# Graph sums one group ahead, exponential factors from the messages product, paced vector work: a graph layer in fp32 on one core

## The chip, the cores and the metric

One core of one Trainium2 chip. The metric is the time of the device in microseconds, the median of the runs. All runs named below are of state fast (undisturbed), and the runs of one kernel agree within 0.4%. The experiments were run in three sittings on three chips, in which the median of the kernel before was 2544.1 (experiments 1 to 4), 2541.0 (5 to 8) and 2543.3 us (9 to 12): a difference of a few us between two of them is noise.

Engine names as in the profile: PE is TensorE's matmuls, PEld its weight loads, DVE VectorE, ACT ScalarE, POOL GpSimd, SP SyncE, which issues the DMAs. PSUM is the memory that TensorE writes its results to; a buffer there is free again when another engine has read it (evacuated it). In the code P = 128 is the number of partitions, NT = 4 the row blocks of a batch, ND = 2 its channel blocks, B = 32, G = 4 batches in a group, NG = 8 groups.

## The reference, cut to what matters

Batches b of 32, each 512 rows of 256 channels. All in fp32.

```python
h = maximum(layernorm(x), 0)
# convolution branch
c = relu(bn1(conv1(h)));  c = bn2(conv2_17_taps(c));  x_conv = relu(h + c)
# graph branch
s    = h @ w_se.T + b_se                        # 3 columns
sq   = sum(s * s, -1)
A    = exp(-(sq[:, None] + sq[None, :] - 2 s @ s.T)) * adj      # 512 x 512
msg  = relu(h @ w_msg.T + b_msg)
x_nmp = A @ msg
# gates: a GRU cell on concat(x_conv, x_nmp) and h, then out = x + cell
```

## The kernel before: the parts that the change touches

Four batches make a group. conv2 of a group is 25 products, each written as two halves (`yield "pe", 1.65`). The rest of the work, here the graph and the gates of the batches of the group before, is a Python generator, and a balance counter `ahead` decides which of the two is emitted next. Each engine is handed its instructions in the order of emission.

The graph stage of one batch, in the order of emission. `positions` of this batch has been emitted in the middle of the gates of the batch before.

```python
def positions(b):                                   # 2 matmuls of 512 columns, four small evacuations
    matmul_sum(ps[:67, :], [(wse[:, i, :], HB[b][:, i, :]) for i in range(ND)])
    ... left[0:3], right[0:3], right[32:35], left[64:67] ...
...
for c in range(NT):                                 # NT = 4
    if c % 2 == 0:
        messages(b, msg, c)
        yield 1.8
    kernel_exp(at, c)                               # one 67-row product of 512 columns, Exp on ScalarE
    yield 0.87
    masked(b, at, c)                                # 4 transposes of the mask, one multiplication on VectorE
    yield 0.55
    if waiting and c % 2:
        finish(*waiting[0], c - 1)                  # output transposes of the batch before
        yield 0.55
```

All four mask row blocks of a batch are one tile of 1 MB, loaded a batch ahead. x has three buffers: three loads are asked for together and their norms follow one after another, so most loads are well ahead of their norm (VectorE waits for an x 6 times, 18.2 us in all). Norm pieces are handed out by `norm_some()`, pieces of the sums of conv2 by `sum_some()`, without a common budget. PSUM: three buffers for conv2, three for the other products, two for transposes.

## Time and profile before

2544.1 us median (2538.2 to 2545.3). What matters for the argument:

| | before |
|---|---|
| TensorE busy | 2386.9 us of 2542.4 |
| TensorE idle | 155 us: 71 in the first 260 us, 63 up to 2250 us, the rest in the tail |
| mean granted clock | 0.973 |
| TensorE work at full clock, by start-to-start times | some 2323 us |
| VectorE busy | 1224.5 us (48%) |

How to read it: span = work at full clock + idle TensorE + the rest of the busy time, most of which the lower clock adds. The lines that carry this stand in the prediction.

### The profile page before, as it was taken

How to read it: one execution, taken by the hardware profiler on the slowest of the kernel's cores; microseconds unless marked ns; L12 is line 12 of the kernel's file. 1: busy time of each engine (PE TensorE's matmuls, PEld its weight loads, DVE VectorE, ACT ScalarE, POOL GpSimd, SP SyncE). 2: the span in 40 equal slices, each digit the busy share in tenths (PEclk: the TensorE clock that was granted, in tenths of full speed). 3: DMA queues.
4: the chain of work that ended last, by engine and by line, in shares of the span. 5: the costliest groups of instructions: out<-in, count | busy, mean ns of one | idle time of the engine just before them, and what ended most of it. 6: DMA issues, size and time to landing. Idle time of an engine off the chain costs nothing.

```text
span 2542.4 us, 20857 instructions
## 1 busy us (share of the span) xinstructions
PE 2386.9 (94%) x8192; PEld 1484.4 (58%) x8192; DVE 1224.5 (48%) x1766; ACT 646.4 (25%) x882; POOL 335.2 (13%) x240
## 2 busy tenths in 40 slices
PE   6678999999999999999999999999999999999998
PEld 4564566655665656655666566665666655665444
DVE  7984543454445444454444554445543454543222
ACT  2332223132132222222212322223212132222222
POOL 1000111111111111112110121100211011111111
PEclk9888999999999999999999999999999999999999
DMA  5233222322232222322223321332222222221110
GB/s 213 114 148 113 85 83 91 116 83 75 83 109 90 91 83 83 124 70 83 87 90 117 99 87 65 106 100 91 91 83 91 91 83 75 91 92 49 42 42 25
DMA packets 108996, 231.15 MB, mean 91 GB/s; under 512 B 8418, under 2 KB 57698, under 8 KB 108258
## 3 DMA queue, kind: packets, MB, share of 16 engines
q1 hardware_dynamic: 108898, 229.82, 26.5%
q8 instruction: 64, 1.05, 0.2%
q14 instruction: 34, 0.28, 0.0%
HBM read 183.13 MB, written 46.66 MB: 90 GB/s over the span
## 4 chain that ended last, share of the span: by engine, by line
PE 83%; DVE 13%; ACT 1%; issue 1%; DMA 1%; POOL 0%; SPq 0%; POOLq 0%; DVEq 0%
PE ps_acc L86 55%; PE ps_c L86 20%; PE ps_acc L488 3%; PE ps_tr L86 2%; DVE x L239 2%; DVE x L242 2%; DVE y L346 2%; PE ps_tr L508 2%; PE ps_tr L496 1%; PE ps_tr L217 1%; DVE at L497 1%; DVE msg L483 1%; DVE z L346 1%; DVE z L353 0%; DVE st L182 0%
## 5 line engine op out<-in xcount | busy, mean ns | idle before, releaser
L86 PEld LDWEIGHTS ps_c<-x,w 128*128 128x128 f32 x3200 | 612.6, 193 | 172.3 <-issue 142.7
L86 PE MATMUL ps_c<-x,w 128*128 128x228 f32 x3200 | 685.1, 360 | 23.7 <-DVE z L368 10.5
L86 PE MATMUL ps_acc<-hTb,whh 128*128 128x512 f32 x768 | 360.2, 594 | 2.0 <-DVE xnmp L502 2.0
L86 PE MATMUL ps_acc<-xconv,wih 128*128 128x512 f32 x768 | 361.3, 593 | 0.0
L86 PE MATMUL ps_acc<-xnmp,wih 128*128 128x512 f32 x768 | 360.6, 592 | 0.0
L599 POOL TENSOR_TENSOR gate_t<-hTb,r 128x512 f32<-128x512 f32 x64 | 88.0, 1375 | 1857.9 <-issue 1260.3
L86 PEld LDWEIGHTS ps_acc<-xnmp,wih 128*128 128x128 f32 x768 | 145.3, 189 | 184.3 <-issue 184.3
L580 DVE SCALAR_TENSOR_TENSOR r<-ps_acc,vec,r 128x512 f32<-128x512 f32 x64 | 48.0, 751 | 413.5 <-ACT r L578 413.5
L86 PEld LDWEIGHTS ps_acc<-xconv,wih 128*128 128x128 f32 x768 | 146.2, 190 | 158.1 <-issue 157.7
L86 PE MATMUL ps_acc<-at,msg 128*128 128x512 f32 x512 | 230.7, 594 | 2.1 <-DVE at L497 2.0
L592 DVE TENSOR_TENSOR r<-ps_acc,r 128x512 f32<-128x512 f32 x64 | 44.3, 692 | 389.8 <-PE ps_acc L86 389.8
L86 PEld LDWEIGHTS ps_acc<-hTb,whh 128*128 128x128 f32 x768 | 143.4, 190 | 124.8 <-issue 119.8
L242 DVE SCALAR_TENSOR_TENSOR x<-x,x 128x471 f32<-128x471 f32 (+1 forms) x184 | 165.1, 897 | 5.1
L86 PEld LDWEIGHTS ps_acc<-at,msg 128*128 128x128 f32 x512 | 97.0, 190 | 109.4 <-issue 103.1
L239 DVE TENSOR_TENSOR x<-x 128x471 f32<-128x471 f32 x200 | 157.5, 804 | 1.4
L86 PE MATMUL ps_acc<-wmsg,hTb 128*128 128x256 f32 x512 | 137.5, 417 | 0.0
L488 PE MATMUL ps_acc<-right,left 67*128 67x512 f32 x256 | 133.9, 604 | 0.0
L588 ACT ACTIVATE z<-ps_acc,brz 128x512 f32<-128x512 f32 x64 | 44.0, 687 | 342.5 <-PE ps_acc L86 342.5
L497 DVE TENSOR_TENSOR at<-ps_tr,at 128x512 f32<-128x512 f32 x128 | 86.5, 687 | 87.5 <-ACT at L489 83.9
L578 ACT ACT_TABLE_LOAD x32 | 41.1, 1283 | 339.2 <-PE ps_acc L86 339.2
L593 ACT ACTIVATE r<-r,vec 128x512 f32<-128x512 f32 x64 | 46.2, 722 | 300.7 <-DVE r L592 300.7
L502 DVE COPY xnmp<-ps_acc 128x512 f32<-128x512 f32 x64 | 44.2, 691 | 158.7 <-PE ps_acc L86 158.6
(90 smaller groups left out, 2213.1 us busy)
## 6 DMA issues: line engine op xcount, KB each, us to landing
w<-wd SPq DMA_DIRECT2D x175, 512.0 KB, 3.4
m_sb<-in_adj_dram SPq DMA_DIRECT2D x32, 1024.0 KB, 6.1
x_sb<-in_x_dram SPq DMA_DIRECT2D x32, 512.0 KB, 6.1
hd<-hT SPq DMA_DIRECT2D x32, 512.0 KB, 3.0
hTb<-hd SPq DMA_DIRECT2D x32, 512.0 KB, 6.7
y<-in_x_dram SPq DMA_DIRECT2D x64, 256.0 KB, 4.0
out_dram<-y SPq DMA_DIRECT2D x64, 256.0 KB, 2.2
wd<-w SPq DMA_DIRECT2D x25, 512.0 KB, 2.6
```

The source lines that it names most:

```text
L86: nc.tensor.matmul(ps, lhsT, rhs, start=(i == 0), stop=(i == len(pairs) - 1))
L239: nc.vector.tensor_tensor(dst, get(a), get(b), op=ALU.subtract)
L242: nc.vector.scalar_tensor_tensor(dst, a, -2.0, b, op0=ALU.mult, op1=ALU.add)
L346: SUMS.append(lambda: nc.vector.tensor_tensor(dst, a, b, op=op))
L488: nc.tensor.matmul(ps, left[:, c * P : (c + 1) * P], right, start=True, stop=True)
L497: nc.vector.tensor_tensor(at[:, c, :], ps, at[:, c, :], op=ALU.mult)
L502: nc.vector.tensor_copy(xnmp[:, d, :], ps)
L508: nc.tensor.transpose(ps[:, j, d * P : (d + 1) * P], o_sb[:, d, (c + j) * P : (c + j + 1) * P], ident)
L580: nc.vector.scalar_tensor_tensor(r, ps_h, vec[:, _COL["b_hh"] + 2 * ND + o : _COL["b_hh"] + 2 * ND + o + 1], r, op0=ALU.add, op1=ALU.mult,)
L592: nc.vector.tensor_tensor(r, ps_n, r, op=ALU.add)
L593: nc.scalar.activation(r, r, AF.Tanh, bias=vec[:, _COL["b_ih"] + 2 * ND + o : _COL["b_ih"] + 2 * ND + o + 1],)
L599: nc.gpsimd.tensor_tensor(t, hT[:, o, :], r, op=ALU.subtract)
```

## The change

Intent: take work off TensorE, the bound, and even out VectorE's work. The positions product disappears into three more columns of the messages product. The four exponent products of a batch, 5 rows deep, run in four row groups of the array at once. For that the graph of a batch is made together with its rows, a group before its gates, and its sums wait in DRAM. A pacer hands out VectorE's work by credit. To fit, x goes from three buffers to two, the mask from one 1 MB tile to three of 256 KB, conv2 from three PSUM buffers to two.

The diff, cut to its core (cuts marked):

```diff
-    cps = ... bufs=3 ...            # conv2's PSUM
-    acc = ... bufs=3 ...
+    cps = ... bufs=2 ...
+    acc = ... bufs=4 ...
-        XS[b] = front.tile([P, NT, D], F32, name="x_sb", bufs=3)
+        XS[b] = front.tile([P, NT, D], F32, name="x_sb", bufs=2)
+    def load_masks(upto):
+        for k in range(len(MS), min(upto, B * NT)):
+            MS[k] = front.tile([P, N], F32, name="m_sb", bufs=3)
+            nc.sync.dma_start(MS[k], adj[k // NT, k % NT * P : (k % NT + 1) * P, :])
 ... (positions and its constants removed; w_se and b_se become columns 256 to 258 of wmsg and bmsg)
+    def kernel_exp(at):
+        pss = [acc.tile([P, N], F32, name="ps_acc") for c in range(NT)]
+        for c in range(NT):
+            k = slice(32 * c, 32 * c + 5)
+            nc.tensor.matmul(
+                pss[c], left[k, :], right[k, :], start=True, stop=True, tile_position=(32 * c, 0)
+            )
+        for c in range(NT):
+            nc.scalar.activation(at[:, c, :], pss[c], AF.Exp)
+    def masked(b, at, n):
+        ... four transposes of MS[b * NT + n], one multiplication ...
+        load_masks(b * NT + n + 4)
+    def begin(b):
+        for d in range(ND):
+            norm_t(b, d)                            # transposes of the normalized x
+            yield 0.55
+        if b + 2 < B:
+            load(b + 2)
+            NORMS[b + 2] = norm(b + 2)              # from here on the pacer may issue it
+    def graph(b, between=()):
+        ... gap(): the next piece of `between`, or a sign that asks for half a conv2 product ...
+        for c in range(NT):
+            messages(b, msg, c)                     # also writes the 3 columns of s
+            yield 0.93
+        factors()                                   # 5 short VectorE instructions
+        yield gap()                                 # filler: in steady state half a conv2 product
+        yield gap()
+        factors_t()                                 # 5 transposes, two copies on ScalarE
+        yield 0.67
+        yield gap()
+        kernel_exp(at)
+        yield 1.2
+        yield from finish_waiting()
+        yield gap()
+        for n in range(NT):
+            masked(b, at, n)
+            yield 0.55
+        yield gap()
+        ... graph sums, copied by ScalarE, stored to DRAM ...
+    def pace(pe):
+        credit = min(credit + pe * 0.8, 4.0)
+        kinds = (sum_next, operand_some, norm_next, prepare_next)
+        while credit > 0:
+            ... issue the next piece of the next kind that has one ...
+            credit -= 0.9
 ... (gates read the sums from DRAM; conv2's weights of all 25 products are made before its first product)
```

## The prediction

> **What bounds the kernel now.** I read the page first: busy shares, then the slices.
>
> ```profile
> PE 2386.9 (94%) x8192; PEld 1484.4 (58%) x8192; DVE 1224.5 (48%) x1766; ACT 646.4 (25%) x882; POOL 335.2 (13%) x240
> ...
> PE   6678999999999999999999999999999999999998
> ...
> DVE  7984543454445444454444554445543454543222
> ...
> PEclk9888999999999999999999999999999999999999
> ```
>
> TensorE is the bound from the fifth slice on. In the first three (190 us) it is 60 to 80% busy and VectorE is the busy one. Next the groups of instructions, TensorE only; the count is of instructions, and one fp32 matmul is two of them.
>
> ```profile
> L86 PE MATMUL ps_c<-x,w 128*128 128x228 f32 x3200 | 685.1, 360 | 23.7 <-DVE z L368 10.5 <-DVE z L370 6.7 <-DVE x L239 3.9
> ...
> L488 PE MATMUL ps_acc<-right,left 67*128 67x512 f32 x256 | 133.9, 604 | 0.0
> ...
> L496 PE MATMUL ps_tr<-ident,m_sb 128*128 128x128 f32 x512 | 77.0, 272 | 0.8 <-DVE at L497 0.8
> L86 PE MATMUL ps_tr<-hTb,wse 128*67 128x512 f32 x128 | 61.9, 607 | 15.5 <-DMA hTb<-hd 15.5
> L508 PE MATMUL ps_tr<-ident,o_sb 128*128 128x128 f32 x256 | 44.7, 303 | 76.2 <-DVE at L497 70.1 <-POOL o_sb L601 5.5
> ```
>
> The means include about 0.17 us of pipeline that overlaps the next matmul, so I take costs from start to start in the timeline. Columns there: start, us, engine, line, operation.
>
> ```profile
> 1001.33 1.70 PE L86 MATMUL ps_c<-x,w 128*128 128x228 f32 x8
> 1002.87 1.88 PE L86 MATMUL ps_tr<-hTb,wse 128*67 128x512 f32 x4
> 1004.58 1.88 PE L86 MATMUL ps_acc<-hTb,whh 128*128 128x512 f32 x4
> ...
> 1053.90 1.02 PE L488 MATMUL ps_acc<-right,left 67*128 67x512 f32 x2
> 1054.76 0.60 PE L496 MATMUL ps_tr<-ident,m_sb 128*128 128x128 f32 x4
> 1055.20 1.02 PE L488 MATMUL ps_acc<-right,left 67*128 67x512 f32 x2
> ```
>
> So four instructions of 512 columns take 1.71 us (0.43 each), eight of 228 take 1.54, one exponent product 0.86, four transposes 0.44. Per batch at full clock: conv2 100 x 0.1925 = 19.25; gates 72 x 0.43 = 30.9; graph sums 16 x 0.43 = 6.9; messages 3.46; conv1 3.44; exponents 4 x 0.86 = 3.44; positions 1.72; mask transposes 1.76; the other transposes 1.76. Sum 72.6 us, by 32 batches 2323 us. The span of 2542 is then 2323 of work, 155 of idle TensorE (2542.4 - 2386.9) and some 64 of busy time at a lower clock.
>
> Where the loss sits: the windows of the first 260 us show 71 us idle and about 15 us lost to the clock, 86 in all. From 260 to 2250 us TensorE waits 63 us, of which 61 are this line:
>
> ```profile
> PE ps_tr L508 <- DVE at L497: 61.1, 18, 6.2
> ```
>
> and a stall costs more than itself. Five-microsecond windows round one of 3.00 us (after the times: TensorE busy, loads, VectorE, ScalarE, GpSimd, clock, DMA share, GB/s):
>
> ```profile
> 885.00:890.00 5.00, 5.00 (x25) 4.21 (x24) 3.44 (x4) 2.23 (x3) 3.78 (x3) 1.00 0.30 105
> 890.00:895.00 5.00, 2.00 (x12) 1.27 (x11) 4.93 (x5) 2.03 (x4) 1.79 (x1) 0.84 0.00 0
> 895.00:900.00 5.00, 5.00 (x15) 4.20 (x15) 3.51 (x12) 0.00 (x0) 0.00 (x0) 0.50 0.16 52
> ```
>
> The clock fell to half for the next 5 us: 2.5 us more lost.
>
> **What the Trainium skill says.** "TensorE: Matmul & The Clock Gate", Part 3, says row tiles at 32-row steps run concurrently, and gives 3.07x for four of K=32, N=512. It also says matmuls start and end strictly in program order. No row tiling is in this trace, so nothing here confirms either. The same page, Part 1, says the clock halves after about 3.4 us without matmul work, and Part 4 that transposes do not count as such work. The windows above agree: a 3.00 us stall between transposes sufficed. "TensorEngine Tiling (Array Packing)", Key Properties, says a change of tiling mode drains TensorE; not shown here, and I allow two pipeline depths of the 0.17 us seen above, 0.35 us a batch.
>
> **The change part by part.**
>
> 1. Positions product removed: 32 x 1.72 = -55 us. Its result now comes from three more columns of the messages product: 259 for 256 columns, +1 us.
>
> 2. Exponents: 32 x 3.44 = 110 us removed. In their place four products of 5 rows in four row groups. An fp32 product is two instructions on the same rows. If all groups overlap fully, a batch costs two passes, 0.86 + 0.35 = 1.2 us. If starts stay in program order (both passes of group 0, then both of group 1), the second pass of one group overlaps only the first of the next: five passes, 5 x 0.43 + 0.2 = 2.35 us. I take 1.7, +54 us.
>
> 3. Five new transposes a batch for the factors: 5 x 0.11 = 0.55, +18 us.
>
> TensorE work: 2323 - 55 + 1 - 110 + 54 + 18 = 2231 us.
>
> 4. Startup. The weights of all 25 conv2 products and the graphs of four batches are now done before the first conv2 product. VectorE in the first stage (to the end of group 0): weight taps 52 us (the sum of their rows); norms of 10 batches by 4.0; graphs of 8 batches by some 6.4 (messages, factors, four masks of 0.69); one group's operands (53 us, an eighth of their rows); most of one group's sums (30 us). About 226 us, and it cannot start on weights before their 4.4 MB have landed, near 20 us. TensorE's work in that stage is 16 graph-row units of the first and second group, about 150, and conv2's 77: also some 227. Neither can be fully busy. I expect 60 idle and 15 of clock loss, 75 against 86.
>
> 5. The middle. The 61 us of boundary waits go, since operand, norm and sum pieces are now issued at 0.8 of TensorE's pace, where before a row of 2.1 us pieces stood ahead of the mask multiplication. But the exponents no longer lie between the mask transposes. Of a batch's four masks, three have buffers ahead; the load of the fourth (256 KB) is issued only after the transposes of the first. The same size lands in 2.1 at least and 3.7 us in the median for the residual loads. Transpose 1 at 0, transpose 2 at 0.44, the third waits for a PSUM buffer until the first multiplication ends (0.6 + 0.69 + wake-up, about 1.45), the fourth for its mask, 0.6 + 2.7 = 3.3. It ends near 3.75 for 1.76 of work: 2.0 lost, and with a piece or two of VectorE work between, 2.2. Four conv2 halves are taken as filler before it, so the balance counter is negative there and no conv2 lies between the masks. Besides: 0.5 waiting for the factors (five short VectorE instructions behind paced ones), 0.3 for the exponentials (a table load of 1.28 and four of 0.6, against 0.88 + 1.54 + 0.88 of cover), and some 1.0 of clock, as 3.75 us with only transposes is the case of the windows above less often. Sum 4.0 a batch by 28 batches outside the startup's first group: 112 us. Other waits of conv2, which has two PSUM buffers instead of three, and of the first load of gates (one of 15.5 us before): 15.
>
> 6. The tail. The last four batches are gates alone. The output transposes now come after one product of 1.72 us of the next batch; they need the last gate: 0.69 + 0.72 + three GpSimd instructions of some 1.5 = 5.9 us. So 4.5 idle three times, with 1 of clock each, about 7 where the last sums and evacuations are waited for, and the 5.5 of the end as before: 29, with clock 33.
>
> 7. Graph sums through DRAM: 64 stores and loads of 256 KB, some 33 MB more on queues that were 26.5% busy: hidden. The copy of 0.69 moves from VectorE to ScalarE, which is 25% busy: no cost.
>
> Sum: 2231 + 75 + 112 + 15 + 33 = 2466 us, a ratio of 0.969 to the 2544 of before.
>
> **The rivals.**
>
> A, the author's arithmetic: row groups fully concurrent (-16 us from my figure) and paced work leaving almost no wait, graphs 1 us a batch (-84), startup 15 better: 2350. For it: VectorE is only 48% busy, and the pace spreads its work. Against: the fourth mask's load, which I see no way round, and the new chain from messages to masks.
>
> B, the waits take the place of the work: masks 3.5 idle and 2.5 of clock each, five passes, startup no better than before. That is +20 for the exponents, +75 for the batches, +15: 2575, slightly slower than before. For it: the clock halved after 3 us, and SyncE's queue is in order, its loads standing behind stores that wait for VectorE. Against: three of four masks are loaded long before.
>
> C, VectorE becomes the bound: pieces issued in bursts of up to 4 us ahead of evacuations, with two conv2 buffers. In the middle VectorE has about 154 us per group of some 290, so it costs some tens of us at most, chiefly at the startup: 2490.
>
> **Range and chances.** I lie between A and B, nearer the middle: 2466 us, 2405 to 2530 eight times in ten. The line for faster is 2493.5. Only 27 us of margin remain, six tenths of a standard spread of 45, so faster 0.68, within 2% 0.30, slower 0.02.
>
> **What would show each step.** Right: no positions group; the exponents' start-to-start near 1.2 to 2.4 us for eight instructions; the fourth mask's transposes waiting for a mask DMA, or the third for the multiplication, in nearly every batch; 61 us of waits before the output transposes gone from the middle; clock in the middle below 1.00 once per batch. Wrong: mask waits under 1 us a batch (then A), the startup's end later than before, conv2 waiting for VectorE's evacuations by more than 40 us (then C), or the exponents at eight passes, 3.4 us, with no overlap at all (+55 us).

## The result, and the profile after

2794.7 us median (2790.8 to 2797.6) against 2544.1: ratio 1.099, interval 1.097 to 1.101. The change made the kernel slower by a tenth; 2466 was predicted.

The page of the changed kernel, busy times and slices:

```profile
PE 2402.3 (86%) x8224; PEld 1516.8 (54%) x8224; DVE 1163.0 (42%) x1989; ACT 639.8 (23%) x930; POOL 301.5 (11%) x239
...
PE   5757878898889888889988889888899899999888
...
PEclk8879988999999999999999999999999999999999
```

TensorE is busy no less than before, though it has less to do. The slices of the middle, 9 before, are now 8 more often than 9. Idle TensorE is 2795.1 - 2402.3 = 393 us against 155; the mean clock fell from 0.973 to 0.923.

The removal itself worked. The exponent products in four row groups, in the timeline (start, us, engine, line, operation):

```profile
1080.13 1.14 PE L522 MATMUL ps_acc<-right,left 5*128 5x512 f32 x8
1081.20 1.09 PE L550 MATMUL ps_tr<-ident,o_sb 128*128 128x128 f32 x8
```

Start to start 1.07 us for all eight instructions, where 3.44 were needed before. So TensorE's work is some 2323 - 55 + 1 - 110 + 34 + 18 = 2211 us by the terms of the prediction, with 32 x 1.07 = 34 for the exponents. The busy time of 2402 is then 191 us more than the work, against 64 before. In sum: work -112, idle +238, the rest of the busy time +127: +253 us, the difference of the two spans (the last term is what is left, so the sum has to close). Added up over windows of 2 us, busy time times missing clock gives 149 us, and 44 for the kernel before: some 105 of the 127 are clock, and the other 22 are not taken apart.

Whom TensorE waited for (us in total, times, longest):

```profile
PE ps_tr L533 <- DVE at L535: 62.1, 28, 5.7
PE ps_c L90 <- issue: 60.3, 11, 6.6
PE ps_tr L508 <- DVE augl L503: 50.1, 17, 5.5
PE ps_c L90 <- ACT n L368: 38.7, 8, 6.6
PE ps_tr L533 <- DMA m_sb<-in_adj_dram: 37.7, 22, 2.6
PE ps_tr L550 <- POOL o_sb L676: 27.4, 9, 5.5
PE ps_c L90 <- DMA w<-wd: 26.2, 1, 26.2
PE ps_tr L533 <- DVE y L554: 23.4, 5, 4.8
```

L533 are the mask transposes: 123 us with all three releasers, 3.9 a batch. L508 is the first transpose of the factors (53 us with all releasers). The conv2 products (ps_c) wait 125 us, mostly in waits of some 5 us. The prediction had 15 us for them, and named more than 40 as a sign of its rival C. "issue" and "ACT n" name no cause there; the timeline of one such wait does:

```profile
968.48 0.39 SPq L97 DMA_DIRECT2D x_sb<-in_x_dram  x1
...
972.79 1.70 PE L90 MATMUL ps_c<-x,w 128*128 128x228 f32 x8
973.57 0.43 DVE L189 BATCH_NORM_STATS2 st<-x_sb 128x6 f32<-128x256 f32 x1 [4.26 <-DMA x_sb<-in_x_dram]
...
976.08 1.02 POOL L146 TENSOR_TENSOR rstd<-veps,mhalf 128x4 f32<-128x4 f32 x1 [5.58 <-DVE veps L145]
977.14 1.38 DVE L197 TENSOR_SCALAR x_sb<-x_sb,mv,rstd 128x256 f32<-128x256 f32 x4 [1.13 <-POOL rstd L146]
...
979.23 0.62 DVE L379 SCALAR_TENSOR_TENSOR z<-n,ps_c 128x456 f32<-128x456 f32 x1
...
979.95 3.38 PE L90 MATMUL ps_c<-x,w 128*128 128x228 f32 x8 [5.46 <-issue]
```

The load of x for batch b+2 is issued at 968.48. The pacer has already put the statistics of that x at the head of VectorE's queue, so VectorE stands for 4.26 us, then stands again 1.13 us for GpSimd. All that was emitted after it waits behind it: the message additions, and the evacuation of the older of conv2's two PSUM buffers (L379). When that is read, at 979.85, conv2 goes on. For the whole kernel the view of waits gives VectorE 94.2 us in 22 waits for this load, the longest 8.7.

The mask stage of another batch:

```profile
1168.89 5.57 SPq L103 DMA_DIRECT2D m_sb<-in_adj_dram  x4
...
1170.38 0.66 PE L533 MATMUL ps_tr<-ident,m_sb 128*128 128x128 f32 x4 [1.09 <-DVE at L535]
...
1173.47 0.63 PE L533 MATMUL ps_tr<-ident,m_sb 128*128 128x128 f32 x4 [2.43 <-DMA m_sb<-in_adj_dram]
```

This is the third and the fourth mask just as predicted: the third waits 1.09 us for the first multiplication, the fourth 2.43 for a load that was asked for at 1168.89. In other batches the multiplication itself stands behind other VectorE work and the wait is up to 5.7 us. And the clock pays after such a stall (columns as in the windows of the prediction):

```profile
1085.00:1090.00 5.00, 1.42 (x7) 1.42 (x8) 4.84 (x9) 1.94 (x4) 0.00 (x0) 0.62 0.10 34
1090.00:1095.00 5.00, 4.10 (x16) 3.15 (x15) 3.18 (x6) 0.00 (x0) 0.00 (x0) 0.50 0.78 235
```

### The profile page after: what moved, and what is told of

It is laid out like the page before. It is cut to its first block, busy times and chain, and to the rows that moved or that the text cites. A ratio compares the mean times of both kernels' runs of the same rounds, so it can differ in the third digit from the quotient of the medians.

```text
span 2795.1 us, 21712 instructions
## 1 busy us (share of the span) xinstructions
PE 2402.3 (86%) x8224; PEld 1516.8 (54%) x8224; DVE 1163.0 (42%) x1989; ACT 639.8 (23%) x930; POOL 301.5 (11%) x239
## 5 line engine op out<-in xcount | busy, mean ns | idle before, releaser
L90 PE MATMUL ps_c<-x,w 128*128 128x228 f32 x3200 | 753.4, 387 | 125.1 <-issue 60.3
L90 PEld LDWEIGHTS ps_c<-x,w 128*128 128x128 f32 x3200 | 657.7, 209 | 237.3 <-issue 142.4
L90 PE MATMUL ps_acc<-xconv,wih 128*128 128x512 f32 x768 | 364.7, 597 | 13.1 <-ACT xconv L629 13.1
L90 PE MATMUL ps_acc<-xnb,wih 128*128 128x512 f32 x768 | 361.6, 593 | 0.0
L90 PEld LDWEIGHTS ps_acc<-xnb,wih 128*128 128x128 f32 x768 | 146.1, 190 | 186.0 <-issue 186.0
L533 PE MATMUL ps_tr<-ident,m_sb 128*128 128x128 f32 x512 | 92.9, 330 | 123.2 <-DVE at L535 62.1
L533 PEld LDWEIGHTS ps_tr<-ident,m_sb 128*128 128x128 f32 x512 | 71.0, 168 | 143.2 <-DVE at L535 90.3
L543 ACT ACTIVATE xnmp<-ps_acc 128x512 f32<-128x512 f32 x64 | 38.2, 597 | 464.3 <-PE ps_acc L90 464.3
L90 PE MATMUL ps_acc<-wmsg,hT 128*128 128x259 f32 x512 | 128.3, 394 | 10.4 <-ACT hT L217 10.4
L237 DVE TENSOR_TENSOR x<-h 128x1415 f32<-128x1415 f32 x40 | 83.2, 2098 | 94.0 <-ACT h L226 94.0
L90 PE MATMUL ps_acc<-hT,w 128*128 128x512 f32 x256 | 118.8, 612 | 0.1
```

The lines of the kernel that those rows point to most:

```text
L90: nc.tensor.matmul(ps, lhsT, rhs, start=(i == 0), stop=(i == len(pairs) - 1))
L237: nc.vector.tensor_tensor(dst, get(a), get(b), op=ALU.subtract)
L533: nc.tensor.transpose(ps[:, c, :], m[:, c * P : (c + 1) * P], ident)
L543: nc.scalar.activation(xnmp, ps, AF.Copy)
```

## The experiments

Theory H: VectorE stands at the head of its queue for the load of x, and what TensorE needs from VectorE waits behind it. Theory M: the graph's chain, above all the four masks with only transposes between them, idles TensorE and drops the clock. Rival B: bursts of the pacer. Rival of buffers: two PSUM buffers for conv2 instead of three.

### 1. The norm handed out later

```diff
             load(b + 2)
-            NORMS[b + 2] = norm(b + 2)
 ... in graph(b), after the masks:
         yield gap()
+        if b + 2 < B:
+            NORMS[b + 2] = norm(b + 2)
         for d in range(ND):
             gather(b, msg, at, d)
```

> One edit to the changed kernel: the norm of batch b+2 is handed to the pacer just before the graph sums of batch b instead of right after its load was asked for. Theory H (VectorE, in order, stands at the head of its queue waiting for x to land, 94 us in 22 waits, and the two conv2 PSUM buffers are not emptied meanwhile): the VectorE wait on the x load falls from 94 to under 15 us, the conv2 waits of 125 us fall to under 45, about 75 us less idle TensorE and some 35 us less clock loss: 2690 us. Rival M (the mask stage and the factor chain are the cost, the x load only moves the wait elsewhere): conv2 waits fall but mask waits grow, 2770 us or more.

Measured: 2611.5 us, ratio to before 1.027 (1.022 to 1.032). That is 183 us off the changed kernel, more than theory H itself expected. VectorE's wait on the load is gone from the view, conv2's waits are 42.9 us (125 before), and the wait for the factors fell too, while those at the masks mostly stayed (108.7 us for 123.2):

```profile
PE ps_tr L533 <- DVE at L535: 62.1, 33, 8.5
PE ps_tr L533 <- DMA m_sb<-in_adj_dram: 46.6, 24, 4.0
...
PE ps_tr L508 <- DVE augl L503: 18.5, 14, 3.8
```

Between the profiled spans (2795.1 and 2614.9) 127 us are idle time (393 to 265.5) and 53 busy time (2402.3 to 2349.4), that is clock: 0.942 for 0.923.

### 2. Filler between the masks

```diff
         for n in range(NT):
             masked(b, at, n)
             yield 0.55
+            yield gap()
```

> One edit to the changed kernel: a half of a conv2 product is put after each of the four masks of a batch, as filler. Theory M (the waits between the four masks, 123 us, and the clock that falls because only transposes run there): mask waits fall to under 50 us, clock from 0.923 to about 0.94, 2690 us. Theory H: the conv2 fillers wait for their PSUM buffers instead, under 40 us gained in all, 2755 us or more.

Measured: 2680.9 us, 114 off, clock 0.934. Waits at the masks fell from 123.2 to 41.4 us, and conv2's stayed at 126. Theory M's number held (2690 expected), so M is a cause beside H; whether the two add, experiment 4 shows.

### 3. Smaller bursts

```diff
-        credit = min(credit + pe * 0.8, 4.0)
+        credit = min(credit + pe * 0.8, 0.9)
```

> One edit to the changed kernel: the pacer's saved credit is capped at 0.9 instead of 4.0, so at most one or two pieces of VectorE work are issued at a time. Theory B (bursts ahead of evacuations, as the three additions of 1.57 us ahead of a mask multiplication): waits for the factors and for the mask multiplication, 53 and 62 us, halve, 2720 us. Theories H and M: no more than 30 us, 2765 us or more.

Measured: 2779.0 us, 16 off. The wait for the multiplications halved (62.1 to 29.9), but those for the mask loads and for the output additions grew (37.7 to 58.0, 23.4 to 42.1): behind one wait stood the next. That for the factors fell only from 53 to 47. Bursts are not the main cause.

### 4. Late norm and filler together

> The edits of the late norm and of the filler together. If theories H and M are separate causes their gains add: about 2580 us, with conv2 waits under 45 us and mask waits under 50 us. If one is only the other's shadow, no better than the better of the two by 20 us.

Measured: 2498.4 us, ratio to before 0.982 (0.979 to 0.985): below the kernel before, but unclear by the line of 2%. The gains add: 183 + 114 = 297, and 2794.7 - 2498.4 = 296. The time is 82 us under the expectation, as experiment 1 gave more than was expected; the masks wait 30.6 us, conv2 47.7, a little over its 45. One group in steady state, from one wait to the same wait a group later, in the changed kernel:

```profile
1076.43:1414.31 337.88, 297.07 (x1029) 188.94 (x1029) 138.23 (x241) 79.07 (x113) 36.26 (x29) 0.93 0.29 95
```

and with both edits:

```profile
950.98:1242.90 291.92, 281.04 (x1029) 176.94 (x1029) 138.22 (x240) 79.33 (x113) 35.58 (x28) 0.99 0.33 110
```

The same 1029 matmuls, the same VectorE time; 46 us less a group, 30 of them idle time and 16 busy time, with the clock at 0.99 for 0.93.

### 5. The tail

The output transposes of the batch before come after the r product instead of before it.

```diff
             yield 1.73
-            if o == 0:
-                yield from finish_waiting()
 ... after the r product:
             yield 5.2
+            if o == 0:
+                yield from finish_waiting()
```

> On the version with the late norm and the filler (2498 us): the output transposes of the batch before come one gate product (5.15 us of TensorE) later in the gates. In the last eight batches they wait 27.4 us for GpSimd's last addition. If that wait and the clock it costs are all there is to the tail: the wait falls to the 5.5 us of the very end, 2465 to 2475 us. If the wait moves to another buffer (the PSUM pair of the transposes, or the output tile): 2490 or more.

Measured: 2478.5 us. The wait for GpSimd fell from 27.4 to the 5.5 of the end, as expected, but the wait for conv2's evacuated sums grew from 13.1 to 24.4: the transposes had covered part of it. 20 us, 3 to 13 short of the expectation; in ratio to before 0.975 (0.971 to 0.979) for 0.982.

### 6. A faster pace in the startup

```diff
     for got in first():
         if got != "gap":
-            pace(got)
+            pace(got * 1.6)
```

> On the version with the late norm and the filler: in the startup alone, before the first conv2 product, the pacer gets 1.6 times the credit. VectorE is 51% busy there and TensorE 61%, and the first conv2 product waits 18 us for weights that are still being made. If the pace itself holds the startup back: the wait for weights goes, 2470 to 2480 us. If VectorE's waits for the conv2 weights' load and for TensorE hold it back: 2490 or more.

Measured: 2488.8 us, 10 off. It lies between the two expectations, and the gain is not clear of noise: the ratio to before is 0.979 (0.976 to 0.982) for 0.982 (0.979 to 0.985). Of the 18 us wait for weights 4.8 are left; the transposes of the factors wait 10 us more for ScalarE instead.

### 7. A third PSUM buffer for conv2, norm where it was

```diff
-    cps ... bufs=2 ...      acc ... bufs=4 ...
+    cps ... bufs=3 ...      acc ... bufs=3 ...
-        pss = [acc.tile([P, N], F32, name="ps_acc") for c in range(NT)]
+        pss = [acc.tile([P, N], F32, name="ps_acc") for c in range(NT - 1)]
+        pss.append(tr.tile([P, N], F32, name="ps_tr"))
```

> On the changed kernel itself (2795 us), the norm where it was: conv2 gets its third PSUM buffer back, and the fourth exponent product uses a buffer of the transposes. Theory H as one of buffers (two conv2 buffers make VectorE's stand into a TensorE wait): conv2 waits of 99 us fall to under 40 and the time to 2700 or less. If the stand of VectorE at the x load is the cause whatever the buffers are: the wait moves to the factors (augl), time 2755 or more.

Measured: 2845.7 us, 51 slower than the changed kernel. Conv2's waits for its evacuations nearly vanished (4.2 us of 99 are left) and came back at the next consumer of VectorE's results:

```profile
PE ps_tr L508 <- DVE augl L503: 135.9, 23, 9.1
PE ps_tr L551 <- ACT at L527: 53.1, 23, 5.2
```

The second line is a cost of this edit's own, as an exponent product now holds a buffer that the output transposes need. So the time alone decides nothing here, but the first line does: with a buffer more for conv2, VectorE's stand is waited for further down the chain.

### 8. The exponents without the groups (wrong result)

On the version with late norm and filler, all four products use row group 0.

```diff
-            k = slice(32 * c, 32 * c + 5)
+            k = slice(0, 5)
-            ... tile_position=(32 * c, 0)
+            ... tile_position=(0, 0)
```

> Wrong result on purpose. On the version with the late norm and the filler: all four exponent products of a batch use row group 0, so they cannot overlap. In the changed kernel eight instructions in four groups took 1.07 us start to start. If overlap is what the groups give: 3.4 us for the eight, 2.35 more a batch, 75 us in all, less what the longer product hides of the exponentials: 2545 to 2575 us. If the short products were fast for their five rows alone, no change: 2498.

Measured: 2630.9 us (the result is off by 0.081), 132 more, where 76 of work were added (82 by the 3.63 us that the eight take here), and 56 over the expected range. So the overlap is what the groups give. The unexpected part is the clock, 0.939 for 0.963. Windows of 2 us over one batch; the serial products run from 1081.1 to 1084.7:

```profile
1083.00:1085.00 2.00, 2.00 (x8) 0.75 (x7) 0.00 (x0) 1.37 (x3) 0.00 (x0) 1.00 0.00 0
1085.00:1087.00 2.00, 2.00 (x11) 1.91 (x10) 1.32 (x3) 0.43 (x1) 0.00 (x0) 0.53 0.00 0
1087.00:1089.00 2.00, 2.00 (x9) 1.75 (x8) 1.95 (x4) 0.00 (x0) 0.00 (x0) 0.61 1.04 291
```

TensorE is busy for all of each window and the clock falls to half right after the 5-row products. The eight transposes that follow them take 1.41 us start to start:

```profile
1084.72 1.62 PE L550 MATMUL ps_tr<-ident,o_sb 128*128 128x128 f32 x8
1086.13 2.90 PE L90 MATMUL ps_c<-x,w 128*128 128x228 f32 x8
```

### 9. The same over all 128 rows (wrong result)

```diff
-            k = slice(32 * c, 32 * c + 5)
-            ... left[k, :], right[k, :], ..., tile_position=(32 * c, 0)
+            ... left, right, ...
```

> Wrong result on purpose. Serial exponent products as in the run of row group 0 alone, but over all 128 rows: the same TensorE time, 3.4 us a batch. That run cost 132 us where 80 of work were added, and its clock fell in the stage after the products with TensorE never idle. If 5-row products count as idleness for the clock: here the clock stays up and the time is 2565 to 2590 us. If the fall has another cause, the transposes beside them: 2620 to 2640 again.

Measured: 2553.0 us (the result is off by 0.43), clock 0.969, with instructions as long as the serial 5-row ones (592 and 588 ns in the median). The eight take 3.44 us start to start, and the eight transposes behind them 0.87, at full clock:

```profile
1042.62 3.60 PE L521 MATMUL ps_acc<-right,left 128*128 128x512 f32 x8
1046.06 1.04 PE L549 MATMUL ps_tr<-ident,o_sb 128*128 128x128 f32 x8
```

So 78 us lie between products of 5 rows and of 128 rows that take nearly the same TensorE time at the same clock (3.63 and 3.44 us a batch, 6 us in all), and they lie in the busy time (2451.7 and 2360.0 us), not in idle time (178 and 191). Here serial 5-row products in one row group do not hold the clock up. Two things changed at once, though: the rows, and the row group, since the 128-row products use the whole array (the values computed differ as well). Which of them the clock answers to was not tried. The gain of the four groups over products on all rows is thus some 2553 - 2498 = 55 us, not the 76 of their TensorE time; the difference is not taken apart further.

### 10. The norm's work in its old place without its wait

On the late-norm version, an additional pass is handed out at the start of batches 8 to 29, where the changed kernel did the norm, over a tile that landed long before and is already normalized. These are 22 passes (not 23, as the expectation says), a stand-in for 22 of the 30 norms that experiment 1 moved.

```diff
             load(b + 2)
+            if b >= 2 * G:
+                NORMS["again", b + 1] = norm(b + 1)
```

> On the version with the late norm alone (2612 us): for batches 8 to 30 an additional norm pass is handed to the pacer where the changed kernel had it, right after the load of x, but over a tile that landed long ago and is already normalized (the result stays right). So the same VectorE work stands in the same place without the wait for x. Theory H (the wait for the load is the cost): 23 passes of 4 us at 47% busy cost little, 2610 to 2650 us. Rival W (4 us of norm work, with its trip to GpSimd, ahead of the message additions is the cost, load or no load): back to 2720 or more.

Measured: 2687.0 us, between H and W: 75 more than the late norm alone. The waits of some 5 us at conv2 did not return (24 us in 16 waits on its evacuations, all but one in the startup at most 1.5 us), but the factors wait again, against 18.5 us without the passes:

```profile
PE ps_tr L508 <- DVE augl L503: 56.4, 24, 5.5
```

So conv2's waits come with the stand at the load, and the waits for the factors with the norm's work alone. The 183 us of experiment 1 are then two things: some 75 for 4 us of norm work, with its trip to GpSimd, ahead of the message additions, and the other 108 for standing at the load. The split is as good as this stand-in is: it leaves out the first batches, and it adds 71 us of VectorE work in all, for which VectorE, 46% busy, has room on the average.

### 11. No mask loaded late (wrong result)

On the late-norm version, three masks are loaded a batch and the third is used twice.

```diff
-        m = MS[b * NT + n]
+        m = MS[b * 3 + min(n, 2)]
 ... (loads counted by threes, the next asked for after masks 0, 1 and 3)
```

> Wrong result on purpose. On the version with the late norm alone: three masks are loaded a batch and the third is used twice, so no mask is ever loaded late. If my fourth mask is what the mask stage waits for: the 46.6 us of waits on mask loads go, with some clock, 2540 to 2560 us. If the multiplications behind other VectorE work set the stage anyway: their wait grows by what the loads' shrinks, 2590 or more.

Measured: 2533.8 us, 78 off, clock 0.961 for 0.942. The result is off by 0.086. TensorE's waits on mask loads at the masks are gone from the view, and that for the multiplications is the same to the tenth, 62.1 us. Between the profiled spans (2614.9 and 2532.4) 43 us are idle time and 40 busy time, that is mostly clock. So the fourth mask of the prediction is real: its load was waited for 46.6 us in the late-norm version, 1.5 a batch, where the prediction's times give 1.4, and the same again went to the clock. (The edit also loads a quarter less of the masks.)

### 12. The edits together

Late norm, filler, later output transposes, faster startup.

> Late norm, filler, later output transposes and faster startup pace together, in search of a version that beats both. If the gains of the last two (20 and 10 us) add: 2465 us; if they overlap: 2480.

Measured: 2476.5 us, ratio 0.974 (0.972 to 0.976): faster than the kernel before, and than the changed one. The startup's gain is lost within the spread (2478.5 without it).

## Why the prediction was wrong

**TensorE's work (parts 1 to 3): right.** The positions group is gone. The exponents took 1.07 us a batch, so 34 us where 54 were allowed: rival A's full overlap was right and the fear of five passes in program order was not. 2211 for 2231. The 1.7 was a middle taken between two cases, neither of which was decided.

**The middle (part 5): the step that failed.** It reads "Sum 4.0 a batch by 28 batches", that is 16 us a group on 279 of work, 295. Measured: 338, which is 15.4 a batch on 276.4 of work (2211 / 8). With the norm late and filler between the masks it is 292, or 3.9 a batch. The 61 us of boundary waits did go, as told. What was in that step:

- "0.5 waiting for the factors (five short VectorE instructions behind paced ones)". Measured 53 us, 1.7 a batch. I took the paced pieces to be work of 0.8 to 2.1 us. One of them was a norm: 4 us with a trip to GpSimd, handed out just ahead of the message additions that the factors need. That alone brings the wait back, load or no load (experiment 10: 56.4 us). With the norm late the factors wait 18.5 us, 0.6 a batch: the number was right without a norm in that place.
- "Other waits of conv2 ... and of the first load of gates: 15." Measured 130 (125 and 5), of which 99 outside the one wait for weights. This is VectorE's stand at an x whose load had only just been issued: conv2 waits 42.9 with the norm late, and 40.6 with the norm's work put back but not the wait (experiment 10). The cut from three x buffers to two stood in the diff and I charged nothing for it. No run gave the third buffer back, so what is shown is the cost of handing out a norm right behind its load, not that of the buffer as such. More than 40 us was my own sign for rival C, and it came; but experiment 7 shows that the two PSUM buffers, of which C spoke, are only where the wait shows, and VectorE is 42% busy.
- The masks: mechanism right, size low. 2.2 idle a batch predicted, 3.85 measured (123.2 / 32). TensorE waits for a mask's load 22 times, as told, 1.2 us a batch. The rest, 2.7 a batch where the prediction's times leave 0.6 to 0.8, is multiplications and output additions behind VectorE's other pieces, up to 5.7 us.
- "some 1.0 of clock". From the end of group 0 to 2400 us, windows of 5 us give 100 us of busy time lost to the clock: 4.2 a batch over 24 batches. The stalls shown above were followed by a stretch at half clock, in a stage of transposes and short products. Experiments 8 and 9 show that the clock falls after serial 5-row products; for the transposes no run shows it apart, and for the four groups at once neither.

**The startup (part 4): also too low.** My terms give 227 + 75 + 16 = 318 to the end of group 0. Its last conv2 product starts at 370.3 us, 52 later. I bounded the stage by VectorE's 226 us of work, but there VectorE is 50 and 62% busy in the first and second 100 us, TensorE 61 and 61%, the clock 0.88 and 0.73. So neither was the bound; the graph's chain has four pieces of filler a batch there and none in the last. With late norm and filler that product starts at 328.6, only 10 over, so the two edits of the middle take most of the excess too. One wait of 26.2 us for the weights is in it (18.3 with both edits), and a faster pace is worth 10 us at most. What makes up the rest is argued from the profile and was not tried.

**The tail (part 6): right in idle time.** In the last four batches TensorE waits 3.9 us three times for GpSimd, 8.9 for GpSimd and for evacuated sums at their start, and 5.5 at the end: 26 us. The prediction's own terms (three times 4.5, 7 and 5.5) are 26 too; its sums of 29, and 33 with clock, were added wrongly and should read 26 and 29.

**DRAM for the graph sums (part 7): right.** No wait on those loads or stores is among TensorE's.

**The rivals.** B, that waits take the place of the work, was the nearest in kind, with 2575; I had it as nearly the extreme and gave slower 0.02. Its argument against itself, "three of four masks are loaded long before", was true, but said nothing of the load of x or of what stands ahead of the multiplications.

## What to carry to other kernels

When a change takes a buffer away from an input, look for the first instruction that reads that input and for what stands behind it on its engine: on VectorE, work handed out before its data was there stopped everything emitted later (94 us in 22 waits). A pacer that counts durations should take up a piece only when its input has had time to land, and not just ahead of a chain that the bound engine waits for: 4 us of norm work there cost some 75 us even with its data at hand. And when short products and transposes are gathered into one stage, put full-row matmuls between them (here 114 us): a stall there was paid a second time in clock.

## What the Trainium skill lacked or had wrong

- "TensorE: Matmul & The Clock Gate", Parts 1 and 4, tell of idle windows and of transposes, not of products over few rows. Here 3.6 us of 5-row products with TensorE never idle were followed by a clock of 0.53 and 0.61, and a kernel with them was 78 us longer than with 128-row products of nearly the same length (clock 0.939 and 0.969). Whether the few rows or the single row group did it is open.
- The same page, Part 3, gives 3.07x for four row groups and says nothing of fp32, where each product here is two instructions on the same rows. Measured: eight instructions in 1.07 us against 3.44 one after the other on 67 or 128 rows, 3.2x. Strict program order of starts did not cost the five passes that I feared.
- "TensorEngine Tiling (Array Packing)", Key Properties, gives no figure for the drain at a change of tiling mode. In the version of experiment 5, eight conv2 instructions before the exponents take 1.64 us start to start where 1.54 is usual, and the exponents 0.21 more than two passes of 0.43: at most 0.31 us a batch.
